# More rows of the gathered table fetched one by one: 36 a group on two issuing engines in place of 8 on one

## The chip, the cores and the metric

The kernel runs on one core of a Trainium2 chip. The metric is the device time of one execution in microseconds (us). Engines: PE = TensorE matmul, PEld = its weight loads, DVE = VectorE, ACT = ScalarE, POOL = GpSimd, SP = SyncE.

## The reference

One layer of graph attention over N = 12500 nodes and 212500 edges (128 features, 8 heads of 16), the edges sorted by their destination:

```python
Q, K, V = x @ WQ, x @ WK, x @ WV                       # N x 128 each, split into 8 heads
Eh = edge_attr @ WE
score = K[src] * Q[dst] / sqrt(16) * Eh                # per edge
score = exp(clip(score.sum(-1), -5, 5))                # one number per edge and head
msg = V[src] * score
h = x + segment_sum(msg, dst) / (segment_sum(score, dst) + 1e-6)
h = batch_norm(h) * gamma + beta
out = layer_norm(x + h)
```

## The kernel before, in words

Edges are cut into 1661 tiles of 128, a row of the chip's 128 partitions for each edge. Eight tiles make a **group** (the last has five); there are 208 groups, each with two windows of up to 64 destination nodes.

**Stage 1** (about the first 80 us) multiplies x with WK and WV and writes the table `kvd` to DRAM: 12500 rows of 1 KB, K and V of a node side by side. Meanwhile POOL gathers rows of x for the first eight groups, which make their K and V themselves.

**Stage 2** is a loop over groups, one iteration per group, software-pipelined by hand: the order of the calls in the loop is the order of the instructions on each engine. For group g the K and V rows of its eight tiles must lie in one of nine buffers (`slot`). They come by indirect DMA issued by POOL (`gather`, L221), one instruction a tile, 128 rows of 1 KB, their numbers taken from `srcs`. A gather for group g + 9 can start when `message(g)` has freed its buffer; in the steady loop gathers are also issued two at a time behind four steps on DVE (`pace`, and `issue`, in the loop).

One iteration on DVE: `products` (L639, K times the query-edge product, two instructions), `scores` (L647), the clip (L657), `both` for the next group (L613), `attn` (L696), `q_rest` (L573), `message` (L663, V times the exponentials), `onehot` (L541 to L544). ACT: `q_hi` (L569, the first part of Q for group g + 3, waits for PE), two exponentials (L658, L659, wait for the clip on DVE), `x_out` (L710), `q_out`, `sums_out`, `eh_out` (L595), `q_window` (L530; every second group a register load of four numbers, L523), `q_mid` (L576). SP loads the edge features of group g + 4 (`ea`, L506, 512 KB, three buffers, so it waits until PE has used group g + 1's), and for every four groups `rbq` (L404).

**Rows one by one.** Of some groups the eighth tile is not gathered by POOL: its 128 rows come by 128 plain DMAs of 1 KB, each with its DRAM address in a register, into a buffer `byrow` of its own (two of them). `row_plan` lists these groups: with n rows fetched an iteration from iteration `FIRST_ROW` on, a tile is complete every 128/n iterations and is used `ROW_LAG` = 2 iterations after its last row was issued. In `fetch_rows` (called once an iteration) SP loads n addresses into registers (L274) and issues n DMAs (L281). They add to one of six semaphores, on which DVE waits in `rows_there` before it uses the tile. Such a group has seven gathers, and its `products`, `scores` and `message` are cut in two, the eighth tile by itself (`parts`).

The loop's start, with the places that the change touches:

```python
    for g in range(NG - 2):
        within(load, g + 4)
        ...
        fetch_rows(g)
        within(q_hi, g + 3)
        within(products, g)
        ...
        within(clip_exp, g)
```

**Stage 3** (about the last 50 us) is the batch norm, the layer norm and the output.

Of the kernel before, what the change touches and what calls it, by code (L numbers as in the profile page):

```python
# [10 lines left out]
U8 = mybir.dt.uint8  # L11
I32 = mybir.dt.int32
# [3 lines left out]
ET = mybir.EngineType  # L16

P = 128
# [4 lines left out]
U = 4  # L23
# [4 lines left out]
EARLY = 3  # L28
RUN = 64
ROWS = P  # L30
FIRST_ROW = 8
LATE = 8
ROW_LAG = 2
SP_ROWS = 8
WORDS = 4
RQ = 4
NSEM = 6
# [40 lines left out]
def gnn_kernel(  # L78
# [31 lines left out]
    consts = ctx.enter_context(tc.tile_pool(name="consts", bufs=1))  # L110
# [129 lines left out]

    by_row, fill = {}, {}
    row_loads = []
    n = SP_ROWS
    row_tiles = row_plan(usizes)
    tot = len(row_tiles) * P
    cols = -(-n // WORDS) * WORDS
    full_rows = tot // n
    blocks = -(-tot // (P * n))
    for q in range(0, full_rows, P):
        row_loads.append((0, q // P * cols, min(P, full_rows - q), n, q * n))  # L250
    if tot % n:
        row_loads.append((full_rows % P, full_rows // P * cols, 1, tot % n, full_rows * n))
    for q in range(-(-tot // n)):
        fill[FIRST_ROW + q] = q
    by_row.update({g: None for g in row_tiles})
    rows_in = [tc.alloc_semaphore(f"rows_in{i}") for i in range(NSEM)]
    row_ids = consts.tile([P, blocks * cols], I32, name="row_ids")
    nc.vector.memset(row_ids, 0)
    kvb = kvd.bitcast(U8).rearrange("n d -> (n d)")

# [1 line left out]
        return [(a, b - 1), (b - 1, b)] if g in by_row and b == G else [(a, b)]  # L262

    def load_row_ids():
        for p, c, m, w, at in row_loads:
            nc.scalar.dma_start(row_ids[p:p + m, c:c + w], bass.AP(
                tensor=rsrc.tensor, offset=rsrc.offset + at, ap=[[n, m], [1, w]]))

    def fetch_rows(g):
        if g not in fill:  # L270
            return
        q = fill[g]
        c = q // P * cols
        _, offs = nc.values_load_multi_w_load_instructions(  # L274
            row_ids[q % P:q % P + 1, c:c + cols], engines=(ET.SP,), min_val=0, max_val=(N - 1) * 8 * P,
            skip_runtime_bounds_check_because="node ids")
        for r, off in zip(range(q * n, min(q * n + n, tot)), offs):
            k = row_tiles[r // P]
            if r % P == 0:
                by_row[k] = rows.tile([P, 1, 2 * P], F32, name="byrow", bufs=2)  # L280
            d = nc.sync.dma_start(by_row[k][r % P:r % P + 1, 0, :].bitcast(U8), kvb[ds(off, 8 * P)].unsqueeze(0))  # L281
# [69 lines left out]
    def within(f, g):  # L351
        return f(g) if 0 <= g < NG else None
# [47 lines left out]
    def load_quad(q):  # L400
        t = late[0].tile([P, RQ, U * P], BF16, name="rbq", bufs=2)
        for h in (0, 1):
            at = ustarts[2 * RQ * q + h] * P
            nc.sync.dma_start(t[h * WN:(h + 1) * WN], bass.AP(  # L404
                tensor=relT.tensor, offset=relT.offset + at, ap=[[0, WN], [G * P, RQ], [1, U * P]]))
        for k in range(RQ):
            RB[RQ * q + k] = t[:, k, :]
# [350 lines left out]
    for q in range(NQ):  # L758
# [13 lines left out]
        k = q - first_step  # L772
# [70 lines left out]
    for g in range(NG - 2):  # L843
        within(load, g + 4)
        within(load_rel, g + 5)
        if (g + 6) % RQ == 0 and (g + 6) // RQ in quads:
            load_quad((g + 6) // RQ)
        fetch_rows(g)
        within(q_hi, g + 3)
        within(products, g)  # L850
        within(q_lo, g + 2)
        within(denom, g - 2)
# [12 lines left out]
        else:  # L865
            left = len(queued)
# [35 lines left out]
        if g == LATE - 2:  # L902
# [3 lines left out]
    g = last - 1  # L906
# [4 lines left out]
                           skip_runtime_bounds_check_because="a count")]  # L911
# [59 lines left out]
    pairs = [[i] for i in range(min(2, NY))] + [list(range(i, min(i + 2, NY))) for i in range(2, NY - 1, 2)]  # L971
# [261 lines left out]
```

## Time and profile before

| what | us |
|---|---|
| median of 3 runs | 2136.09 (2130.42 to 2140.72) |
| the profiled execution: its own time | 2129.71 |
| its span, first to last instruction | 2127.9 |
| busy: PE, DVE, POOL, ACT | 1710.7, 1592.0, 1594.6, 672.2 |
| indirect gathers on POOL | 64 of x, 1585 of `kvd` |
| rows one by one | 1536, that is 12 tiles |

The mean granted TensorE clock of that execution is 0.917. A line of instructions in the profile gives the source line, the engine, the operation, output <- inputs, how many, then busy us, mean ns of one, the idle time just before them, and what ended that idle time. A timeline line gives the start and the duration in us, and in brackets the idle time before it with what ended it ("issue": nothing that the profile shows). "SPq" and "ACTq" are the instructions of the engine's instruction queue: register loads, moves and the issue of DMAs.

### The profile page before, as it was taken

To read this page: it belongs to the slowest core of one execution; us is meant where nothing else is said; L and a number is where in the kernel's file an instruction comes from. 1 tells how busy PE (TensorE), PEld (TensorE's weight loads), DVE (VectorE), ACT (ScalarE), POOL (GpSimd) and SP (SyncE) were. 2 spreads that over 40 slices of the span, in tenths; PEclk is the share of its full clock that TensorE was granted. 3 is DMA by queue.
4 is the path that set the end of the run, shared out by engine and by line. 5 is a ranking of instruction groups with operands and counts; after the bars stand their busy time and mean duration, and the time that the engine had idled before them with its cause. 6 is when DMAs were issued, how large, how long until landed. Compare 5 with 4: busy or idle time off the path is not lost.

```text
span 2127.9 us, 34950 instructions
## 1 busy us (share of the span) xinstructions
PE 1710.7 (80%) x9414; PEld 1105.5 (52%) x9414; DVE 1592.0 (75%) x3593; ACT 672.2 (32%) x2688; POOL 1594.6 (75%) x1685
## 2 busy tenths in 40 slices
PE   8889999777787787787777877787777777777787
PEld 7566566444554454454444554454544444455457
DVE  4559999777777777777777777767777777777687
ACT  3344343322322322322222323223223223223226
POOL 7777777777777777777777777777777777777775
PEclk9999999998998999999898899989898999898889
DMA  9856666565565555565565565565565565565574
GB/s 305 283 183 189 203 198 195 175 175 165 175 176 165 175 177 165 175 178 165 177 174 164 178 175 176 165 175 167 175 178 169 171 177 166 173 180 172 169 237 128
DMA packets 175395, 386.65 MB, mean 182 GB/s; under 512 B 37518, under 2 KB 91831, under 8 KB 175191
## 3 DMA queue, kind: packets, MB, share of 16 engines
q0 software_dynamic: 78128, 212.05, 33.9%
q1 hardware_dynamic: 92900, 169.50, 25.6%
q10 hardware_dynamic: 4163, 2.78, 0.5%
q8 instruction: 78, 1.28, 0.2%
q14 instruction: 126, 1.03, 0.2%
HBM read 364.57 MB, written 19.63 MB: 181 GB/s over the span
## 4 chain that ended last, share of the span: by engine, by line
DVE 32%; DMA 30%; issue 14%; POOL 11%; PE 10%; ACT 1%; DVEq 0%; SPq 0%; POOLq 0%; ACTq 0%
DMA slot<-kvd,srcs 29%; POOL slot L221 11%; DVE s L647 9%; DVE wt L613 6%; DVE slot L639 6%; DVE msg L663 3%; PE ps_a L680 2%; DVE q L579 2%; DVE s L657 1%; PE ps_e L588 1%; PE ps_t L345 1%; DVE rz L692 1%; PE ps_e L725 1%; PE ps_q L725 1%; PE ps_t L621 1%
## 5 line engine op out<-in xcount | busy, mean ns | idle before, releaser
L221 POOL DMA_INDIRECT slot<-kvd,srcs x1585 | 1506.3, 950 | 486.7 <-issue 324.5
L639 DVE TENSOR_TENSOR slot<-slot,ps_t 128x512 f32<-128x512 f32 (+1 forms) x410 | 274.4, 678 | 422.5 <-DMA slot<-kvd,srcs 380.8
L621 PE MATMUL ps_t<-ident,wt 128*128 128x128 f32 x1661 | 282.6, 313 | 365.0 <-DVE wt L613 363.7
L680 PE MATMUL ps_a<-msg,oh 128*128 128x136 f32 (+1 forms) x3322 | 526.5, 298 | 0.5 <-DVE msg L663 0.5
L621 PEld LDWEIGHTS ps_t<-ident,wt 128*128 128x128 f32 x1661 | 212.9, 159 | 538.9 <-issue 472.8
L680 PEld LDWEIGHTS ps_a<-msg,oh 128*128 128x128 f32 (+1 forms) x3322 | 427.6, 171 | 79.5 <-issue 53.4
L658 ACT ACTIVATE ps_m<-s 128x64 f32<-128x64 f32 (+1 forms) x209 | 47.5, 227 | 1095.1 <-DVE s L657 1046.1
L588 PE MATMUL ps_e<-ea,w_e 128*128 128x512 f32 x832 | 390.6, 591 | 0.7 <-ACT wt L595 0.7
L613 DVE TENSOR_TENSOR wt<-wt,ps_q 128x512 f32<-128x512 f32 x416 | 264.6, 676 | 2.6 <-PE ps_q L603 2.6
L663 DVE TENSOR_TENSOR msg<-slot,ps_m 128x1024 f32<-128x1024 f32 (+3 forms) x209 | 246.9, 1183 | 0.4 <-ACT ps_m L658 0.3
L647 DVE TENSOR_REDUCE s<-slot 128x64 f32<-128x1024 f32 (+2 forms) x208 | 246.8, 1187 | 0.1
L595 ACT ACTIVATE wt<-ps_e 128x512 f32<-128x512 f32 x416 | 233.4, 618 | 12.9 <-PE ps_e L588 12.9
L603 PE MATMUL ps_q<-ot,q 64*128 64x512 bf16 x1248 | 210.9, 453 | 0.0
L588 PEld LDWEIGHTS ps_e<-ea,w_e 128*128 128x128 f32 x832 | 142.6, 190 | 100.4 <-issue 98.5
L541 DVE TENSOR_TENSOR oh<-ps_m,rel_i 128x512 f32<-128x512 f32 x208 | 142.0, 683 | 11.2 <-PE ps_a L680 11.2
L569 ACT ACTIVATE q<-qs 128x128 bf16<-128x128 f32 x208 | 64.3, 309 | 216.8 <-PE ps_q L603 183.8
L705 PEld LDWEIGHTS ps_a<-ident,at 128*128 128x128 f32 x408 | 71.3, 218 | 110.8 <-issue 53.5
L705 PE MATMUL ps_a<-ident,at 128*128 128x128 f32 x408 | 114.2, 367 | 2.5 <-DVE relrow L395 2.3
L710 ACT ACTIVATE hx<-ps_a 128x64 f32 x408 | 88.4, 217 | 43.3 <-PE ps_a L680 36.3
L530 ACT ACTIVATE xw<-hx 128x64 f32 x416 | 88.0, 278 | 10.5 <-DMA hx<-xT 10.2
L603 PEld LDWEIGHTS <-q 64*128 64x128 bf16 x1248 | 48.7, 102 | 79.4 <-issue 62.2
L561 PE MATMUL ps_a<-w_q,xw 128*128 128x128 f32 x416 | 88.6, 298 | 0.6 <-ACT qs L565 0.4
(180 smaller groups left out, 1632.6 us busy)
## 6 DMA issues: line engine op xcount, KB each, us to landing
ea<-eaT SPq DMA_DIRECT2D x207, 512.0 KB
slot<-kvd,srcs POOLq DMA_INDIRECT x1585
byrow<-kvd SPq DMA_DIRECT2D x1536, 1.0 KB
rbq<-relT SPq DMA_DIRECT2D x94, 256.0 KB
kvd<-slot SPq DMA_DIRECT2D x12, 512.0 KB
kvd<-t SPq DMA_DIRECT2D x12, 512.0 KB
slot<-xT SPq DMA_DIRECT2D x24, 256.0 KB
out<-o SPq DMA_DIRECT2D x23, 256.0 KB
```

Of the source, the lines that this page charges most:

```text
L221: return nc.gpsimd.indirect_dma_start(out=out, out_offset=None, in_=table, in_offset=bass.IndirectOffsetOnAxis(ap=srcs[:, e:e + 1], axis=0))
L541: nc.vector.tensor_tensor(one, iota_ps[:, None, :].to_broadcast([P, n, P]), r[:, :n, None].to_broadcast([P, n, P]), op=OP.is_equal)
L588: nc.tensor.matmul(eh, w_e, EA[g][:, a:b, :].rearrange("p a b -> p (a b)"), start=True, stop=True)
L595: nc.scalar.activation(t[:, :(b - a) * P], EH[g][h], AF.Copy)
L603: nc.tensor.matmul(QE[g][h], Q3[g][r, k, :], OT[g][r, :(b - a) * P], start=(k == 0), stop=(k == 2))
L613: nc.vector.tensor_tensor(t, t, QE[g][h], op=OP.mult)
L621: nc.tensor.transpose(ps[:, j, :], WT[g][h][:, j * P:(j + 1) * P], ident)
L639: step = nc.vector.tensor_tensor(kv, kv, PW[g][i][:, c - a:d - a, :], op=OP.mult)
L647: step = nc.vector.tensor_reduce(SS[g][:, a:b, :], KV[g](a, b, 0).rearrange("p t (h d) -> p t h d", d=DH), axis=AX.X, op=OP.add)
L663: step = nc.vector.tensor_tensor(MSG[g][:, a:b, :P].rearrange("p t (h d) -> p t h d", d=DH), KV[g](a, b, P).rearrange("p t (h d) -> p t h ...
L680: nc.tensor.matmul(AGG[g][WN if j >= n else 0:], OH[g][j], MSG[g][:, j, :], start=(j == 0), stop=(j == n - 1))
L705: nc.tensor.matmul(ps, AT[g], ident, start=True, stop=False)
```

## The change

36 rows an iteration in place of 8, from iteration 6 in place of 8. SP issues 20 of them where it issued 8; ACT issues the other 16, behind `q_hi` and ahead of the exponentials. `row_plan` then gives 55 tiles in place of 12: groups 11, 15, 18, 22, ... 203 in place of 25, 41, ... 201. POOL gathers 43 tiles fewer. The addresses lie in another order, two fetches to a partition, SP's and ACT's apart.

```diff
-FIRST_ROW = 8
+FIRST_ROW = 6
 LATE = 8
 ROW_LAG = 2
-SP_ROWS = 8
+SP_ROWS = 20
+ACT_ROWS = 16
...
-    full, n = sizes.count(U) // 2, SP_ROWS
+    full, n = sizes.count(U) // 2, SP_ROWS + ACT_ROWS
...
+    def offsets(q, et):
+        c, w, m = (0, sp_step, SP_ROWS) if et == ET.SP else (act_at, act_step, ACT_ROWS)
+        _, offs = nc.values_load_multi_w_load_instructions(
+            row_ids[q // 2:q // 2 + 1, c + q % 2 * w:c + (q % 2 + 1) * w], engines=(et,), min_val=0,
+            max_val=(N - 1) * 8 * P, skip_runtime_bounds_check_because="node ids")
+        return offs[:m]
+
-    def fetch_rows(g):
+    def fetch_rows(g, et, a, b):
         if g not in fill:
             return
-        q = fill[g]
-        c = q // P * cols
-        _, offs = nc.values_load_multi_w_load_instructions(
-            row_ids[q % P:q % P + 1, c:c + cols], engines=(ET.SP,), min_val=0, max_val=(N - 1) * 8 * P,
-            skip_runtime_bounds_check_because="node ids")
-        for r, off in zip(range(q * n, min(q * n + n, tot)), offs):
+        at = fill[g] * n
+        b = min(b, tot - at)
+        if b <= a:
+            return
+        eng = {ET.SP: nc.sync, ET.Activation: nc.scalar}[et]
+        for r, off in zip(range(at + a, at + b), offsets(fill[g], et)):
             k = row_tiles[r // P]
             if r % P == 0:
                 by_row[k] = rows.tile([P, 1, 2 * P], F32, name="byrow", bufs=2)
-            d = nc.sync.dma_start(by_row[k][r % P:r % P + 1, 0, :].bitcast(U8), kvb[ds(off, 8 * P)].unsqueeze(0))
+            d = eng.dma_start(by_row[k][r % P:r % P + 1, 0, :].bitcast(U8), kvb[ds(off, 8 * P)].unsqueeze(0))
...
-        fetch_rows(g)
+        fetch_rows(g, ET.SP, 0, SP_ROWS)
         within(q_hi, g + 3)
+        fetch_rows(g, ET.Activation, SP_ROWS, SP_ROWS + ACT_ROWS)
         within(products, g)
```

What moves, engine by engine. Source lines behind the change stand up to 19 higher than before (L281 is now L299, L569 is L587, L658 is L676).

SP in the middle of the loop, one iteration before the change (`ea` are edge features, `rbq` the loads for four groups, `row_ids` the addresses):

```order
L506 DMA ea<-eaT 128x1024
L404 DMA rbq<-relT 64x4x512 x2
L274 TENSOR_LOAD row_ids
L281 DMA byrow<-kvd 1x1024 x8
L506 DMA ea<-eaT 128x1024
```

and after it:

```order
L524 DMA ea<-eaT 128x1024
L422 DMA rbq<-relT 64x4x512 x2
L282 TENSOR_LOAD row_ids
L299 DMA byrow<-kvd 1x1024 x20
L524 DMA ea<-eaT 128x1024
```

The order is the same; one register load now fills 20 registers, and 20 DMAs stand ahead of the next `ea`.

ACT in the middle of the loop, from `q_mid` to `x_out`, before the change (`q` are the parts of Q, `ps_m<-s` and `msg<-s` the two exponentials):

```order
L576 ACTIVATE q_3251<-qs 128x128
L569 ACTIVATE q_3361<-qs 128x128
L658 ACTIVATE ps_m<-s 128x64
L659 ACTIVATE msg<-s 128x8x8
L710 ISA
L710 ACTIVATE hx<-ps_a 128x64
```

and after it:

```order
L594 ACTIVATE q_4504<-qs 128x128
L587 ACTIVATE q_4711<-qs 128x128
L282 TENSOR_LOAD row_ids
L299 DMA byrow<-kvd 1x1024 x16
L676 ACTIVATE ps_m<-s 128x64
L677 ACTIVATE msg<-s 128x8x8
L728 ISA
L728 ACTIVATE hx<-ps_a 128x64
```

A register load of 16 numbers and 16 DMAs now stand between `q_hi` and the exponentials.

POOL, the gathers of groups 9 to 13, one buffer a row, before the change:

```order
L221 DMA slot_628<-kvd,srcs 128x256 x8
L221 DMA slot_777<-kvd,srcs 128x256 x8
L221 DMA slot_864<-kvd,srcs 128x256 x8
L221 DMA slot_924<-kvd,srcs 128x256 x8
L221 DMA slot_989<-kvd,srcs 128x256 x8
```

and after it:

```order
L222 DMA slot_628<-kvd,srcs 128x256 x8
L222 DMA slot_777<-kvd,srcs 128x256 x8
L222 DMA slot_864<-kvd,srcs 128x256 x7
L222 DMA slot_924<-kvd,srcs 128x256 x8
L222 DMA slot_988<-kvd,srcs 128x256 x8
```

Group 11 has lost a gather; before, group 25 was the first with seven.

More of the change, by code (lines that the diff above doesn't have):

```diff
@@ L242, in gnn_kernel @@
     row_loads = []
-    n = SP_ROWS
+    n = SP_ROWS + ACT_ROWS
     row_tiles = row_plan(usizes)
     tot = len(row_tiles) * P
[L246 to L252, printed above, removed]
+    sp_step = -(-SP_ROWS // WORDS) * WORDS
+    act_at = 2 * sp_step
+    act_step = -(-ACT_ROWS // WORDS) * WORDS
+    pairs = tot // (2 * n)
+    assert pairs < P
+    row_loads.append((0, 0, [[2 * n, pairs], [n, 2], [1, SP_ROWS]], 0, sp_step))
+    row_loads.append((0, act_at, [[2 * n, pairs], [n, 2], [1, ACT_ROWS]], SP_ROWS, act_step))
+    for k in (0, 1):
+        left = tot - 2 * n * pairs - k * n
+        at = (2 * pairs + k) * n
+        for c, a, m in ((k * sp_step, 0, SP_ROWS), (act_at + k * act_step, SP_ROWS, ACT_ROWS)):
+            m = min(m, left - a)
+            if m > 0:
+                row_loads.append((pairs, c, [[1, 1], [1, 1], [1, m]], at + a, m))
     for q in range(-(-tot // n)):
         fill[FIRST_ROW + q] = q
+    cols = act_at + 2 * act_step
     by_row.update({g: None for g in row_tiles})
     rows_in = [tc.alloc_semaphore(f"rows_in{i}") for i in range(NSEM)]
-    row_ids = consts.tile([P, blocks * cols], I32, name="row_ids")
+    row_ids = consts.tile([P, cols], I32, name="row_ids")
     nc.vector.memset(row_ids, 0)
```

8 lines of the change are left out of this document (5 added, 3 removed).

## The prediction

> **What bounds the kernel now.** I read the page first (busy shares, costliest groups), then the waits, then timelines of single engines. On the page these groups matter; the first number behind the bar is busy us, the second the mean ns of one, then the idle time before them.
>
> ```profile
> PE 1710.7 (80%) x9414; PEld 1105.5 (52%) x9414; DVE 1592.0 (75%) x3593; ACT 672.2 (32%) x2688; POOL 1594.6 (75%) x1685
> L221 POOL DMA_INDIRECT slot<-kvd,srcs x1585 | 1506.3, 950 | 486.7 <-issue 324.5
> L639 DVE TENSOR_TENSOR slot<-slot,ps_t 128x512 f32<-128x512 f32 (+1 forms) x410 | 274.4, 678 | 422.5 <-DMA slot<-kvd,srcs 380.8
> L658 ACT ACTIVATE ps_m<-s 128x64 f32<-128x64 f32 (+1 forms) x209 | 47.5, 227 | 1095.1 <-DVE s L657 1046.1
> ```
>
> By share of busy time PE would be the bound. But DVE's one large wait is for gathers (380.8 us), and POOL's idle time, 486.7 us over 1585 gathers, is 0.307 us each, nearly the same ahead of every one. So I looked at POOL in order of time, at three places: early, in the middle, at the end.
>
> ```profile
> 172.20 0.98 POOL L221 DMA_INDIRECT slot<-kvd,srcs  x1 [0.30 <-issue]
> 177.18 0.94 POOL L221 DMA_INDIRECT slot<-kvd,srcs  x1 [4.00 <-DVE msg L663]
> ...
> 1005.27 0.94 POOL L221 DMA_INDIRECT slot<-kvd,srcs  x1 [0.30 <-issue]
> 1006.52 0.96 POOL L221 DMA_INDIRECT slot<-kvd,srcs  x1 [0.30 <-issue]
> ...
> 2074.97 0.95 POOL L221 DMA_INDIRECT slot<-kvd,srcs  x1 [0.30 <-DVE rz L689]
> ```
>
> A gather starts every 1.25 us, waiting for nobody but once: at 177.18 the nine buffers are full and POOL waits 4.0 us for `message` of group 8 to free one. 1585 x 1.25 = 1981 us, and the last gather starts at 2074.97, 53 us before the span ends: **POOL's rate of issuing gathers is the bound**, 10.0 us for eight. How far the other engines are from it is seen where DVE still has gathered groups in store (first row) and in the middle (second row):
>
> ```profile
> 300.00:400.00 100.00, 92.84 (x550) 57.20 (x548) 93.40 (x212) 36.87 (x155) 75.70 (x80) 1.00 0.66 196
> 1000.00:1200.00 200.00, 157.86 (x843) 99.84 (x844) 146.75 (x334) 57.27 (x237) 151.32 (x159) 0.88 0.57 169
> ```
>
> PE and DVE (first and third busy time) are 93% busy in the one and 79% and 73% in the other.
>
> **The gain.** 43 gathers fewer, 43 x 1.25 = 53.8 us. Two of them don't count: those of groups 11 and 15 are issued ahead of the wait at 177.18, which ends when `message(8)` does, so POOL only waits longer. 41 x 1.25 = **51.3 us**. An average iteration then has 8 - 36/128 = 7.72 gathers, 9.65 us. Whether that is had depends on what issues the rows.
>
> **SP.** These are its instructions for a row (min/median/max ns), its register loads of eight numbers and of one, and two stretches of its timeline.
>
> ```profile
> L281 SPq MOVE byrow<-kvd x1536: 29/29/38, 172.4 to 1998.5; - x192
> L281 SPq DMA_DIRECT2D byrow<-kvd x1536: 221/228/310, 172.5 to 1998.5; - x192
> L274 SPq TENSOR_LOAD <-row_ids x192: 698/735/1020, 171.4 to 1995.1; - x192
> L910 SPq TENSOR_LOAD <-bad_i x1: 471/471/471, 2069.4 to 2069.4; - x1
> ...
> 211.01 1.25 SPq L404 DMA_DIRECT2D rbq<-relT  x2
> ...
> 1010.14 0.36 SPq L506 DMA_DIRECT2D ea<-eaT  x1
> 1011.41 2.52 SPq L281 DMA_DIRECT2D byrow<-kvd  x8
> ```
>
> Eight rows take 2.52 us, 0.32 each. From the start of `ea` to the first row is 1.27 us with a load of eight numbers. A load of 20 is not in the trace: from 0.471 (one) and 0.735 (eight) along a line it is 1.19, in proportion to eight 1.84; I take the line, since it has both rows. An iteration of SP is then 1.27 + 0.45 + 20 x 0.32 + 1.25/4 = **8.4 us** (9.1 by the other end), under 9.65. It costs nothing as long as that holds; the next `ea` goes out up to an iteration late, and is used three iterations after its issue. The last rows of a tile are issued two iterations before their use.
>
> **ACT.** It has no such row yet. Its DMAs and register loads (four numbers, one number) are:
>
> ```profile
> L396 ACTq DMA_DIRECT2D relT<-relrow x15: 235/327/586, 32.7 to 1971.5; - x15
> L523 ACTq TENSOR_LOAD <-base_i x104: 304/308/985, 33.8 to 2029.0; - x104
> L910 ACTq TENSOR_LOAD <-bad_i x1: 292/292/292, 2066.9 to 2066.9; - x1
> ```
>
> A row on ACT costs between SP's 0.32 and 0.586 + 0.09 = 0.68 us. ACT's quickest DMA, 0.235 us, is so close to SP's 0.228 that I take 0.32. The load of 16 numbers lies between 0.3 (the line through 0.292 and 0.308 hardly rises) and 16/4 x 0.308 = 1.2; I take 0.45. The block is 16 x 0.32 + 0.45 = **5.6 us**, 11 at the far end. The Trainium skill (DMA: Bandwidth & Descriptors, Latency and other measured facts) gives a `tensor_load` a floor of about 0.6 us; ACT's rows of 0.29 and 0.31 are under it, and by the floor the block would be 5.8.
>
> Behind the block wait both exponentials, and for them `message` on DVE. What covers it is ACT's wait for the clip, from `q_hi` (L569) to the exponential (L658), in iterations 6, 7 and 8, in the stretch bound by DVE, and in the steady one:
>
> ```profile
> 149.81 0.31 ACT L569 ACTIVATE q<-qs 128x128 bf16<-128x128 f32 x1 [0.61 <-PE ps_q L603]
> 151.82 0.23 ACT L658 ACTIVATE ps_m<-s 128x64 f32<-128x64 f32 x1 [1.69 <-DVE rz L692]
> ...
> 164.79 0.31 ACT L569 ACTIVATE q<-qs 128x128 bf16<-128x128 f32 x1 [0.61 <-PE ps_q L603]
> 166.83 0.23 ACT L658 ACTIVATE ps_m<-s 128x64 f32<-128x64 f32 x1 [1.73 <-DVE rz L692]
> ...
> 171.52 0.31 ACT L569 ACTIVATE q<-qs 128x128 bf16<-128x128 f32 x1 [0.61 <-PE ps_q L603]
> 173.83 0.23 ACT L658 ACTIVATE ps_m<-s 128x64 f32<-128x64 f32 x1 [2.00 <-DVE s L657]
> ...
> 213.31 0.31 ACT L569 ACTIVATE q<-qs 128x128 bf16<-128x128 f32 x1 [0.54 <-PE ps_q L603]
> 217.32 0.23 ACT L658 ACTIVATE ps_m<-s 128x64 f32<-128x64 f32 x1 [3.71 <-DVE s L657]
> 220.44 0.31 ACT L569 ACTIVATE q<-qs 128x128 bf16<-128x128 f32 x1 [0.55 <-PE ps_q L603]
> 1003.83 0.31 ACT L569 ACTIVATE q<-qs 128x128 bf16<-128x128 f32 x1 [1.90 <-PE ps_q L603]
> 1009.38 0.23 ACT L658 ACTIVATE ps_m<-s 128x64 f32<-128x64 f32 x1 [5.24 <-DVE s L657]
> ```
>
> ```profile
> 219.19 1.22 DVE L663 TENSOR_TENSOR msg<-slot,ps_m 128x1024 f32<-128x1024 f32 x1
> ```
>
> The windows are 2.0, 2.0, 2.3, 4.0 and 5.5 us. DVE starts `message` 1.6 us after the exponential's end (217.32 to 219.19), busy with other groups' work, so 1.6 us more is covered. From about iteration 15 on, 4.0 + 1.6 = 5.6 covers the block just so; in the steady stretch there is more. If it were not covered, ACT's loop would be 2.6 us (217.32 to 220.44, less the 0.55 wait) plus the block, 8.2 us, still under 9.65. But in **iterations 6 to 8** it sticks out, and `message(8)` frees the buffer for which POOL waits. Iteration 6 loses 5.6 - 2.0 = 3.6 (ACT still makes K and V of group 7 there, so the slack does not help), iteration 7 5.6 - 2.0 - 1.6 = 2.0, iteration 8 5.6 - 2.3 - 1.6 = 1.7: **+7 us** of POOL's wait, once. The bounds are 0 (PE and DVE absorb it) and 11 (a load of 1.2 us: 0.8 to 1.2 more in each).
>
> **DVE.** Each of 43 groups more is cut in two, three times:
>
> ```profile
> L647 DVE TENSOR_REDUCE s<-slot 128x64 f32<-128x1024 f32 x190 | 230.4, 1212 | 0.0
> L647 DVE TENSOR_REDUCE s<-slot 128x56 f32<-128x896 f32 x12 | 12.9, 1077 | 0.0
> L647 DVE TENSOR_REDUCE s<-byrow 128x8 f32<-128x128 f32 x12 | 3.3, 274 | 0.0
> ```
>
> 1.077 + 0.274 - 1.212 = 0.14 us, three times, 0.42 a group, 18 us in all. It lies in DVE's 380.8 us of waiting for gathers and costs nothing; with that cover gone it would cost the 18.
>
> **The sum:** 2129.7 - 51.3 + 7 = 2085.4 on the profiled execution. The median of the runs shown is 6 us higher, within their spread; I predict **2086**, and for this case 2076 (53.8 gained, nothing lost) to 2095.
>
> **Rivals.**
>
> *Two engines issuing at once stretch each row* (slower). No stretch of the trace has SP and ACT issuing single rows together. SP decides first: if it is the bound, the 196 fetches begin near 150 us and the last is used some 80 us before the end (three iterations of 7.1 and the 53 us after the last gather, and a landing), so the time is 230 + 196 S. It passes 2085 at S = 9.46, a row at 0.37 us, and 2130 at S = 9.69, a row at 0.385. At 0.40 S is 10.0 and the time **2190**. On ACT the same happens from 0.41 us a row (block 7.0, loop 9.6). For: SP's margin is only 0.05 us a row, and single issues of 0.31 in place of 0.228 occur. Against: 228 is the median, next to a maximum of 310, while POOL and the `ea` stream run beside it.
>
> *A part of it*: rows at 0.37 to 0.385, or a 1.84 us load besides; the gain is half eaten, 2095 to 2128.
>
> *One DMA engine for all rows* (slower). Each row is one descriptor, and might always go through the same one of the 16 DMA engines. The queues' load:
>
> ```profile
> q0 software_dynamic: 78128, 212.05, 33.9%
> q1 hardware_dynamic: 92900, 169.50, 25.6%
> q10 hardware_dynamic: 4163, 2.78, 0.5%
> ```
>
> 33.9% and 25.6% of 10.0 us are 6.0 us an iteration on each engine. A packet takes 0.5% x 16 x 2128/4163 = 0.041 us (q10, 0.67 KB) to 0.094 (q1, 1.8 KB), and a row of 1 KB lies between: 36 add 1.5 to 3.4 us, 7.5 to 9.4 in all, under 9.65. From 0.10 us a row that engine would set the pace, since every gather ends when its slowest part has landed; at 0.12, 10.3 us, 230 + 196 x 10.3 = 2250. The Trainium skill (DMA: Bandwidth & Descriptors, Why a DMA increments its semaphore by 16 and not by 1) says that a transfer whose outer dimension is 1 uses one engine, on these queues the lowest-numbered. The profile gives only the mean of the 16, so no row here shows it.
>
> *The gathers saved are not on the path*: against it stands POOL's unbroken row of starts; it would give 2130 or, with DVE's 18 us, 2148.
>
> **How the numbers follow.** The forecast has 0.70; part of the gain 0.12; slower by two issuers 0.12, by one DMA engine 0.04; off the path 0.02. The range 2070 to 2125 takes in the first (with the runs' spread of 5 us below) and most of the second. About 0.5%, some 11 us, is what a measurement of this kernel tells from no change: faster by over that 0.78, within it 0.07, slower 0.15.
>
> **What would show it.** Right: 1542 gathers from `kvd`, still 1.25 us apart, the last near 2030; POOL's wait near 177 grown from 4 us to over 10; SP's 20 rows in 6.4 us and ACT's block in 5.6; the exponential's wait shrunk to about 0 to 2 us. Wrong: POOL waiting for `message` all along, SP without idle time, or DVE waiting for rows at L639. What would upset the forecast most is a row that costs 0.06 us more when both queues are in use.

## The result, and the profile after

The changed kernel takes **2136.12 us** (median of 12 runs, 2133.39 to 2141.62) against 2136.47 us for the kernel before (12 runs, 2130.42 to 2140.72): a ratio of 1.0004, 95% interval 0.9993 to 1.0015. No change, where 2086 was predicted. The profiled execution of the changed kernel took 2141.62 us (span 2139.8), 11.9 us more than that of before; these two executions lie at opposite ends of the runs' spread, and a second profile of the changed kernel (2133.67 us) stands beside them below. Some of the runs told below were made under conditions in which the kernel before itself takes 2730 to 2758 us; each ratio is to the kernel before run beside it on the same chip, and those runs stand apart, at the end of the experiments.

On the page of the changed kernel POOL has 43 gathers fewer and still the same end. Its idle time ahead of the gathers has grown from 486.7 to 533.7 us:

```profile
PE 1711.0 (80%) x9414; PEld 1105.5 (52%) x9414; DVE 1598.6 (75%) x3722; ACT 650.0 (30%) x2688; POOL 1559.5 (73%) x1642
L222 POOL DMA_INDIRECT slot<-kvd,srcs x1542 | 1470.7, 954 | 533.7 <-issue 310.7
```

The chain that ended last now runs through the issue of rows on both engines and through the rows' own DMAs, neither of which was among its larger shares before:

```profile
DMA slot<-kvd,srcs 26%; SPq L299 9%; DMA byrow<-kvd 8%; ACTq L299 7%; POOL slot L222 6%; DVE s L665 3%; SPq L282 2%; DVE slot L657 2%; DVE wt L631 2%; PE ps_a L698 2%; PE ps_t L639 2%; DVE msg L681 1%; PE ps_t L363 1%; PE ps_q L621 1%; ACTq L282 1%
```

Where the time went is read best from the count of POOL's instructions in three stretches (200 to 300 us has 80 in both kernels). The count stands behind the fifth busy time, in brackets. First the kernel before, then the changed one:

```profile
100.00:200.00 100.00, 91.94 (x538) 64.53 (x538) 67.45 (x159) 46.15 (x144) 72.85 (x78) 0.97 0.60 184
300.00:1200.00 900.00, 717.82 (x3917) 450.46 (x3916) 686.76 (x1556) 268.19 (x1115) 681.51 (x717) 0.91 0.59 174
1200.00:2000.00 800.00, 624.58 (x3386) 390.96 (x3385) 593.01 (x1330) 233.74 (x972) 605.56 (x639) 0.91 0.58 173
```

```profile
100.00:200.00 100.00, 78.20 (x410) 56.32 (x409) 47.39 (x113) 36.41 (x108) 55.49 (x59) 0.87 0.44 132
300.00:1200.00 900.00, 720.38 (x4010) 455.82 (x4010) 705.81 (x1657) 263.36 (x1141) 657.11 (x690) 0.93 0.64 176
1200.00:2000.00 800.00, 639.06 (x3443) 396.49 (x3441) 604.06 (x1408) 229.35 (x984) 603.35 (x633) 0.92 0.63 176
```

19 gathers fewer fit into the first stretch, 27 into the second and 6 into the third: 52 x 1.25 = 65 us of waiting that were not there before, against 43 x 1.25 = 53.8 us saved. The difference is, within a gather, the 11.9 us by which the last gather starts later (2074.97 before, 2086.9 now).

**The first stretch.** Three waits of POOL make it up; before there was one, of 4.0 us:

```profile
162.66 0.94 POOL L222 DMA_INDIRECT slot<-kvd,srcs  x1 [10.12 <-DVE s L665]
177.74 0.94 POOL L222 DMA_INDIRECT slot<-kvd,srcs  x1 [6.63 <-issue]
198.31 0.94 POOL L222 DMA_INDIRECT slot<-kvd,srcs  x1 [10.77 <-DVE msg L681]
```

Two things stand behind them. The addresses are loaded at 108 us by ACT in five DMAs: two of 97 partitions, which took 1.44 and 3.41 us to issue, and three of one partition, 2.72, 0.24 and 0.26 (before: two, of 128 and 64 partitions, 0.34 and 0.53 us). The Q part and the exponential behind them had to wait. Besides, ACT's block of rows sits between `q_hi` (L587) and the exponential (L676) when nothing covers it:

```profile
108.44 1.44 ACTq L276 DMA_DIRECT2D row_ids<-rsrc  x1
109.93 6.75 ACTq L276 DMA_DIRECT2D row_ids<-rsrc  x4
118.96 0.31 ACT L587 ACTIVATE q<-qs 128x128 bf16<-128x128 f32 x1 [9.68 <-DMA row_ids<-rsrc]
...
161.47 0.31 ACT L587 ACTIVATE q<-qs 128x128 bf16<-128x128 f32 x1 [0.61 <-PE ps_q L621]
162.71 5.32 ACTq L299 DMA_DIRECT2D byrow<-kvd  x16
168.08 0.23 ACT L676 ACTIVATE ps_m<-s 128x64 f32<-128x64 f32 x1 [6.30 <-issue]
```

From 161.47 to 168.08 are 6.6 us; in the same iteration before it was 2.0.

**The second stretch** has no long wait but many short ones. Two rows of POOL's waits in 300 to 1200 us, before and after (in all, times, longest):

```profile
POOL slot L221 <- issue: 139.0, 456, 0.3
POOL slot L221 <- DMA slot<-kvd,srcs: 15.8, 52, 0.3
```

```profile
POOL slot L222 <- issue: 128.5, 407, 2.1
POOL slot L222 <- DMA slot<-kvd,srcs: 37.8, 97, 1.2
```

Before, no wait is over 0.3 us, which is POOL's own pause between gathers. Now it waits up to 1.2 us for *earlier gathers to land*: its gathers take turns on eight semaphores, so each one waits for the gather eight before it, issued 10.0 us earlier. How late they land, the trace's semaphore increments tell. A gather raises its semaphore sixteen times. The trace lacks some increments, so these are medians over the gathers that have at least fourteen of them, in 600 to 900 us, in us after the gather's start:

```
                 last increment but one   last increment
kernel before             2.75                 2.83
changed kernel            3.00                 8.48   (one in ten: 9.9 or more)
```

Fifteen sixteenths come nearly as before and **one comes 5.6 us later**. The same holds for the edge features (`ea`): the last increment but one comes at 4.04 us, the last at 13.23 (before 3.45 and 3.65). One part of sixteen is behind in such transfers. That this is one DMA engine is read from it, and agrees with the rule of the Trainium skill that the prediction named (DMA: Bandwidth & Descriptors, Why a DMA increments its semaphore by 16 and not by 1): it gives a `[1, 1]` transfer to one engine, on these queues the lowest-numbered, and in the trace a row is a `[1, 1]` transfer of 1 KB. No view names the engine.

How much of POOL's loss stands behind a late landing can be counted in the traces. In 300 to 1200 us POOL's starts slip by 36.8 us (counting those over 0.06 us late). Of these, 24.3 us are starts 0.26 or 0.76 us (within 0.02) behind the landing of the gather eight before. Another 8.4 us are seven single starts, each 106 gathers after the one before; five of them stand 3.34 us behind that landing. In the second profile of this kernel, below, it is 18.6 and 8.7 of 32.9 us (at five of the same starts, four of them at 3.34). What is left, 4.1 and 5.6 us, is not much more than all that the kernel before has: 3.9 us, none of it behind a landing. Why every 106th start needs longer, the profile does not say; in the kernel before these starts come 4.1 us or more after the landing, and one of the six there is late, by 0.15 us.

The rows were issued at the pace that was forecast; the loads of their addresses took longer than taken. Minimum, median and maximum in ns:

```profile
L299 SPq DMA_DIRECT2D byrow<-kvd x3920: 217/228/2910, 163.1 to 2048.7; - x196
L299 ACTq DMA_DIRECT2D byrow<-kvd x3120: 226/232/692, 162.7 to 2029.8; - x195
L282 SPq TENSOR_LOAD <-row_ids x196: 1382/1449/1782, 161.4 to 2040.8; - x196
L282 ACTq TENSOR_LOAD <-row_ids x195: 1012/1199/1302, 161.5 to 2023.0; - x195
```

Two things that the prediction had listed as signs of failure are there too: DVE waits for rows, and SP hardly waits for PE any more (1072.1 us before). Beside them DVE waits for ACT's exponentials, 100 times (0.3 us in all before):

```profile
DVE byrow L657 <- DVEq L306: 91.1, 18, 10.4
SPq L524 <- PE ps_e L606: 144.5, 44, 15.3
DVE msg L681 <- ACT ps_m L676: 108.2, 100, 3.4
```

Whether they cost time, these rows do not say; that was the question for the experiments.

### The profile page after: what moved, and what is told of

Same layout as the page of the kernel before. It is cut to its first block, busy times and chain, and to the rows that moved or that the text cites. A ratio compares the mean times of both kernels' runs of the same rounds, so it can differ in the third digit from the quotient of the medians.

```text
span 2139.8 us, 46352 instructions
## 1 busy us (share of the span) xinstructions
PE 1711.0 (80%) x9414; PEld 1105.5 (52%) x9414; DVE 1598.6 (75%) x3722; ACT 650.0 (30%) x2688; POOL 1559.5 (73%) x1642
## 4 chain that ended last, share of the span: by engine, by line
DMA 36%; DVE 13%; SPq 12%; issue 11%; PE 11%; ACTq 8%; POOL 6%; ACT 3%; DVEq 0%; POOLq 0%
DMA slot<-kvd,srcs 26%; SPq L299 9%; DMA byrow<-kvd 8%; ACTq L299 7%; POOL slot L222 6%; DVE s L665 3%; SPq L282 2%; DVE slot L657 2%; DVE wt L631 2%; PE ps_a L698 2%; PE ps_t L639 2%; DVE msg L681 1%; PE ps_t L363 1%; PE ps_q L621 1%; ACTq L282 1%
## 5 line engine op out<-in xcount | busy, mean ns | idle before, releaser
L222 POOL DMA_INDIRECT slot<-kvd,srcs x1542 | 1470.7, 954 | 533.7 <-issue 310.7
L639 PE MATMUL ps_t<-ident,wt 128*128 128x128 f32 x1661 | 261.7, 299 | 258.8 <-DVE wt L631 257.9
L676 ACT ACTIVATE ps_m<-s 128x64 f32<-128x64 f32 (+1 forms) x209 | 47.5, 227 | 1255.1 <-DVE qs L591 374.9
L639 PEld LDWEIGHTS ps_t<-ident,wt 128*128 128x128 f32 x1661 | 204.4, 152 | 416.0 <-issue 341.6
L657 DVE TENSOR_TENSOR slot<-slot,ps_t 128x512 f32<-128x512 f32 (+1 forms) x410 | 261.5, 661 | 203.7 <-DMA slot<-kvd,srcs 155.4
L681 DVE TENSOR_TENSOR msg<-slot,ps_m 128x1024 f32<-128x1024 f32 (+3 forms) x209 | 241.8, 1158 | 105.5 <-ACT ps_m L676 104.8
L665 DVE TENSOR_REDUCE s<-slot 128x64 f32<-128x1024 f32 (+2 forms) x208 | 240.5, 1157 | 0.1
L621 PE MATMUL ps_q<-ot,q 64*128 64x512 bf16 x1248 | 198.8, 430 | 0.0
L579 PE MATMUL ps_a<-w_q,xw 128*128 128x128 f32 x416 | 100.3, 326 | 57.0 <-ACT xw L548 56.1
L579 PEld LDWEIGHTS ps_a<-w_q,xw 128*128 128x128 f32 x416 | 70.6, 212 | 80.5 <-ACT xw L548 78.6
L587 ACT ACTIVATE q<-qs 128x128 bf16<-128x128 f32 x208 | 67.8, 326 | 113.9 <-PE ps_q L621 81.6
L714 DVE SCALAR_TENSOR_TENSOR at<-os,keep,rz 128x128 f32<-128x128 f32 x208 | 71.4, 343 | 33.5 <-PE ps_a L723 32.8
```

What stands on the lines that cost most here:

```text
L222: return nc.gpsimd.indirect_dma_start(out=out, out_offset=None, in_=table, in_offset=bass.IndirectOffsetOnAxis(ap=srcs[:, e:e + 1], axis=0))
L621: nc.tensor.matmul(QE[g][h], Q3[g][r, k, :], OT[g][r, :(b - a) * P], start=(k == 0), stop=(k == 2))
L639: nc.tensor.transpose(ps[:, j, :], WT[g][h][:, j * P:(j + 1) * P], ident)
L657: step = nc.vector.tensor_tensor(kv, kv, PW[g][i][:, c - a:d - a, :], op=OP.mult)
L665: step = nc.vector.tensor_reduce(SS[g][:, a:b, :], KV[g](a, b, 0).rearrange("p t (h d) -> p t h d", d=DH), axis=AX.X, op=OP.add)
L681: step = nc.vector.tensor_tensor(MSG[g][:, a:b, :P].rearrange("p t (h d) -> p t h d", d=DH), KV[g](a, b, P).rearrange("p t (h d) -> p t h ...
```

## The experiments

Theories. **One engine**: all single rows go through one DMA engine, it falls behind, delivers its sixteenth of each gather late, and POOL waits for the gather eight before. **Issuers**: SP (without idle time, 20 rows) and ACT (late with the exponentials, 16 rows) hold the groups back, and the late landing is beside the point. For the first stretch both say the same.

**The changed kernel again.**

> The changed kernel once more, unaltered, in the conditions of the other runs, where the kernel before takes 2734 to 2738 us. One-engine theory and issuer theory alike leave open what it takes there; from the nearest runs (rows from group 10 on: 1.152 to 1.154 of the kernel before) it should take 1.14 to 1.17 of it, if the chip is of that kind, and 0.997 to 1.003 of it, if the kernel before takes 2136 us again.

2135.56 us, ratio 1.0016 (1.0004 to 1.0027): as in the result. Its profile has the same waits: POOL's first stretch, 27.0 us beyond its pace in 100 to 300 us, and 33.3 in 300 to 1200 (27.6 and 38.5 in the first profile).

**Late start, whole rows and half rows.** Both begin the rows at group 10; the row fetches are then 192, two DMAs of 96 partitions load all addresses, and there are 54 tiles.

```diff
-FIRST_ROW = 6
+FIRST_ROW = 10
...
-    row_loads.append((0, 0, [[2 * n, pairs], [n, 2], [1, SP_ROWS]], 0, sp_step))
-    row_loads.append((0, act_at, [[2 * n, pairs], [n, 2], [1, ACT_ROWS]], SP_ROWS, act_step))
+    even = pairs // 16 * 16
+    for p, m in ((0, even), (even, pairs - even)):
+        if m:
+            at = 2 * n * p
+            row_loads.append((p, 0, [[2 * n, m], [n, 2], [1, SP_ROWS]], at, sp_step))
+            row_loads.append((p, act_at, [[2 * n, m], [n, 2], [1, ACT_ROWS]], at + SP_ROWS, act_step))
```

> The change with rows from group 10 on and addresses in pieces of 96 and 1 partitions, whole rows of 1 KB. Where the kernel before takes 2132 to 2137 us: if bytes don't count for the one DMA engine, the same as with half rows, 0.990 of the kernel before (2105 to 2115); if they do, 2116 to 2125. Where it takes 2735 to 2758: 1.15 of it.

With half rows besides:

```diff
-                by_row[k] = rows.tile([P, 1, 2 * P], F32, name="byrow", bufs=2)
-            d = eng.dma_start(by_row[k][r % P:r % P + 1, 0, :].bitcast(U8), kvb[ds(off, 8 * P)].unsqueeze(0))
+                by_row[k] = rows.tile([P, 1, P], F32, name="byrow", bufs=2)
+            d = eng.dma_start(by_row[k][r % P:r % P + 1, 0, :].bitcast(U8), kvb[ds(off, 4 * P)].unsqueeze(0))
...
-                                      by_row[g][:, :, c:c + n])
+                                      by_row[g][:, :, :n])
```

> The change with rows of 512 bytes in place of 1 KB (of a row only the key's half is fetched and stands for the value's half too; the value's half is left out), with rows from group 10 on and with addresses in pieces of 96 and 1 partitions. Both theories: GpSimd's waits of 100 to 200 us fall from 27 us to under 8. One-engine theory: gathers land after 5 to 6 us in place of 8.5 and GpSimd's extra time in 300 to 1200 us falls from 4 to 5 us per 100 us to under 1.5; in all 2136 - 20 - 30 = 2086 (2075 to 2100). Issuer theory: the middle stays as it is: 2115 (2108 to 2125). This holds where the kernel before takes 2132 to 2137 us; where it takes 2735 to 2758, the ratio is 1.15 to 1.17.

Whole rows: 2110.97 us, ratio 0.9893 (0.9869 to 0.9916). Half rows: 2109.91 us, ratio 0.9904 (0.9888 to 0.9921). Whole rows in the three stretches, then half rows in the second:

```profile
100.00:200.00 100.00, 89.40 (x502) 63.23 (x502) 64.00 (x151) 43.23 (x132) 69.80 (x74) 0.94 0.58 170
300.00:1200.00 900.00, 724.35 (x4029) 457.77 (x4028) 712.50 (x1668) 265.93 (x1152) 666.02 (x699) 0.93 0.64 177
1200.00:2000.00 800.00, 635.56 (x3482) 394.25 (x3480) 608.45 (x1416) 230.29 (x992) 602.77 (x635) 0.93 0.63 178
```

```profile
300.00:1200.00 900.00, 729.84 (x4043) 459.67 (x4044) 713.58 (x1674) 266.50 (x1152) 669.00 (x702) 0.94 0.65 176
```

The first stretch has 74 gathers again (59 in the change, 78 before): the early waits were on the path, 15 x 1.25 = 19 us of the 24. Most of the rest of the 25 us by which this kernel is faster than the changed one lies in the second stretch, where it loses 26.3 us against 38.5 and 33.3 in the two profiles of the change. The address loads now take ACT 0.69 and 0.84 us, and POOL's one long wait there is 5.9 us:

```profile
110.96 0.69 ACTq L280 DMA_DIRECT2D row_ids<-rsrc  x1
111.69 0.84 ACTq L280 DMA_DIRECT2D row_ids<-rsrc  x1
```

```profile
180.17 0.94 POOL L222 DMA_INDIRECT slot<-kvd,srcs  x1 [5.94 <-DVE msg L685]
```

How much of the 19 us is the addresses and how much the start was not taken apart. The second stretch stays short of gathers, 699 and 702 against 717: the one-engine forecast for half rows (2086, gathers landing after 5 to 6 us) was missed, and 2109.91 us lies in the range that the issuer theory gave (2108 to 2125). Gathers land after 8.40 us (whole) and 7.93 us (half) in 600 to 900 us, so the bytes of the rows are not what makes their landing late; whole rows came within the range given for that case (2105 to 2115). The waits still stand behind landings: counted as above, 16.0 and 4.8 of 26.0 us with whole rows, 13.3 and 4.0 of 23.3 with half rows.

How late it is, is seen in ACT's rows too, each of which is one packet of 1 KB (or 512 bytes) on ACT's own queue, so that the k-th issue belongs to the k-th packet. A packet of 1 KB takes 46 ns and its semaphore 9. But from issue to the packet's start pass 6.64 us in the changed kernel (median, 600 to 900 us), 6.69 with the late start and 5.35 with half rows. So a row of 55 ns stands in a queue for over 6 us, and halving its bytes shortens that by a fifth. What it stands behind, the gathers' packets of 4 KB with 164 ns each or the other loads, no run shows. By its work that engine is not full: an estimate from these rows is 36 x 0.055 = 2.0 us an iteration beside the 6.0 that the prediction worked out, 8.0 of some 10.

**20 rows by SP alone.** The kernel before with:

```diff
-FIRST_ROW = 8
+FIRST_ROW = 6
...
-SP_ROWS = 8
+SP_ROWS = 20
```

> The kernel before with 20 rows a group by SyncE, none by ScalarE (31 tiles, first rows at group 6). Where the kernel before takes 2132 to 2137 us: if the one DMA engine falls behind only while two engines issue rows together (0.16 us a row, against 0.18 that it can land), one issuer's 0.32 us a row leaves it free: gathers land after 3 to 4 us, GpSimd's extra time in 300 to 1200 us is under 10 us, and 19 gathers x 1.25 = 24 us are saved: 2110 to 2118. If SyncE's 20 rows hold the groups back, the extra time stays near 25 us: 2125 to 2136. Where the kernel before takes 2735 to 2758: 1.11 of it.

2114.09 us, ratio 0.9901 (0.9877 to 0.9924); 31 tiles. Waits and the second stretch:

```profile
SPq L506 <- PE ps_e L588: 150.0, 49, 15.4
```

```profile
DVE byrow L639 <- DVEq L288: 75.4, 12, 12.7
```

```profile
300.00:1200.00 900.00, 733.19 (x4083) 462.86 (x4081) 714.68 (x1648) 286.79 (x1158) 681.75 (x717) 0.92 0.64 180
```

This settles the SP half of the issuer theory, which had forecast 2125 to 2136. SP has as little idle time as in the change (150.0 us of waiting against 144.5), DVE waits for rows nearly as long (75.4 us), and yet POOL issues 717 gathers, as before. Gathers land after 3.23 us, and time and landing are within what the one-engine theory gave. Both signs were harmless by themselves.

**14 rows by SP and 14 by ACT**, with the late start:

```diff
-SP_ROWS = 20
-ACT_ROWS = 16
+SP_ROWS = 14
+ACT_ROWS = 14
```

> 14 rows by SyncE and 14 by ScalarE (some 42 tiles), rows from group 10 on, addresses in pieces of 96 and 1 partitions. Where the kernel before takes 2132 to 2137 us: one-engine theory by two issuers: the bursts overlap for 4.5 us in place of 5.4 to 6.4, gathers land after 5 to 7 us, extra time in the middle 8 to 15 us, 30 gathers x 1.25 = 37.5 saved: 2108 to 2116. SyncE theory: SyncE has 2 us more a group than it needs, extra time under 5 us: 2098 to 2107. Where the kernel before takes 2735 to 2758: 1.02 of it.

**2100.32 us**, ratio 0.9836 (0.9812 to 0.9859): the fastest, 42 tiles. Second stretch, and POOL's waits in it:

```profile
300.00:1200.00 900.00, 735.23 (x4012) 460.55 (x4011) 710.33 (x1646) 267.54 (x1148) 681.79 (x715) 0.92 0.64 179
```

```profile
POOL slot L222 <- issue: 136.1, 446, 0.3
POOL slot L222 <- DMA slot<-kvd,srcs: 25.4, 83, 0.3
```

No wait is over 0.3 us in these rows; 715 gathers. Gathers land after 6.06 us in 300 to 600 us and 3.74 from 600 to 900; an ACT row's packet starts 3.85 and 1.20 us after its issue. So two issuers at once, and a block of 14 rows between `q_hi` and the exponential (DVE waits 43.3 us for exponentials in the whole run), cost POOL hardly anything: 6.9 us in this stretch against 3.7 before. The time is in the range of the SyncE theory (the SP half of the issuer theory: 2098 to 2107) and under that of the one-engine theory (2108 to 2116), which had sized the lateness too large. The SyncE theory itself does not survive the 20 rows by SP.

All kernels in one table: gathers and rows, POOL's time beyond 1.251 us a gather by stretch, and the landing in 600 to 900 us.

| kernel | POOL's gathers of `kvd` | 100 to 300 | 300 to 1200 | 1200 on | last increment |
|---|---|---|---|---|---|
| before | 1585 | 4.6 | 3.7 | 1.7 | 2.83 |
| changed | 1542 | 27.6 | 38.5 | 9.0 | 8.48 |
| late start | 1543 | 9.0 | 26.3 | 7.6 | 8.40 |
| late start, half rows | 1543 | 8.0 | 23.3 | 8.7 | 7.93 |
| 20 by SP | 1566 | 8.1 | 4.6 | 3.4 | 3.23 |
| 14 + 14, late start | 1555 | 8.0 | 6.9 | 5.7 | 3.74 |

By this table the start of the last gather is accounted for: for 14 + 14, 30 x 1.251 = 37.5 saved and 10.6 lost, 26.9; its last gather starts at 2048.1, 26.8 us earlier than before.

**When the wait fades.** DVE has a store of gathered groups at first. In the changed kernel `scores` of a group starts 73 us (median) after the start of the group's last gather in 300 to 400 us, 21 us in 1000 to 1200 and 19 after that; in the kernel before it is 26 us in 300 to 400 and 14 from then on. The slips go with the store: 3 to 6 us per 100 us up to 1000 us in both profiles of the change, at most 2.3 from 1200 on, while the landing falls from 8.5 to some 7 us. With half rows the store is used up by 700 to 800 us, and the slips, up to 7 us per 100 before, are at most 2.6 from there on. With 14 + 14 it is used up by 400 to 500 us.

So the table's last column sets kernels with a store beside kernels without. While it lasts, in 300 to 400 us, gathers land after 7.6 us with 14 + 14 and 8.3 in the change; without it, from 1200 to 1600 us, after 3.7 and 7.1. With 20 rows by SP it is about 3 us all along. The lateness thus grows with the rows with the store and without it, and the wait appears where it nears POOL's 10.0 us.

**Under the other conditions** the kernel before takes 2730 to 2758 us, at a granted clock of about 0.81. What differs is seen with 20 rows by SP, first under those conditions, then under the result's:

```profile
1002.37 10.42 SPq L281 DMA_DIRECT2D byrow<-kvd  x20
1013.50 0.00 SPq L506 DMA_DIRECT2D ea<-eaT  x1
1013.51 1.55 SPq L404 DMA_DIRECT2D rbq<-relT  x2
1016.60 8.96 SPq L281 DMA_DIRECT2D byrow<-kvd  x20
```

```profile
1008.89 6.37 SPq L281 DMA_DIRECT2D byrow<-kvd  x20
1015.36 0.36 SPq L506 DMA_DIRECT2D ea<-eaT  x1
1017.33 6.79 SPq L281 DMA_DIRECT2D byrow<-kvd  x20
```

A row's median issue is 228 ns in both, but here single instructions, register moves too, take 0.7 or 1.4 us now and then (562 of SP's 3970 moves over 0.2 us; in the changed kernel's own trace none of 3922). Twenty rows then take 11.1 us (median, 6.4 under the result's conditions), and SP waits for PE only 35.9 us: there, it seems, every instruction more on an issuing queue is paid. Gathers land after 2.8 to 4.2 us (medians of the few, some 36 to 56 a run, that have fourteen increments in the trace), so the runs say nothing of the theories, and the expectations, where they were written for the result's conditions, fail:

> 20 rows an iteration, all issued by SP from iteration 6, none by ACT: 30 tiles by rows, so 18 gathers fewer than in the kernel before, 22.5 us of POOL's time. Theory ACT (the block of rows on ACT is what ate the gain): ACT is free, so nearly all of it is had, about 2115 us, with gathers still landing late. Theory engine (all rows go through one DMA engine, which is late with its part of every gather): with 20 rows in place of 36 the gathers' last part lands after some 4 to 6 us in place of 8.5, POOL waits for no landing, about 2115 too; the two differ in the landing time. Theory off the path: 2136.

> 36 rows as in the changed kernel, but from iteration 10 on in place of 6 (54 tiles in place of 55), and the addresses come from DRAM by transfers of 96 partitions in place of 97. Theory early (a third of the loss is POOL waiting for buffers before 200 us, since ACT issues address loads for 8 us in iteration 2 and rows while it still makes K and V): POOL's waits before 220 us fall from 26.6 us to under 8, and the time by 15 to 20 us, to about 2118. Theory engine: the early loss goes, but the slow middle stays at some 40 us of POOL waiting, so it stops at 2115 or above. If the middle sets the pace by itself, the time stays near 2136.

> The change with rows of 512 bytes in place of 1 KB: of a row only the key's half is fetched and stands for the value's half too (the value's half is left out). The number of rows, the instructions of SyncE and ScalarE and the work of VectorE stay. One-engine theory: the one DMA engine moves 18 KB a group less, gathers land after 5 to 6 us in place of 8.5, row issues of 0.5 to 2.9 us go away, and most of the 40 us that GpSimd loses between 300 and 1200 us comes back: 2095 to 2112. Issuer theory: SyncE's 20 rows still take 6.4 us and ScalarE's block 6.6: 2130 to 2140.

> The change with rows of 512 bytes in place of 1 KB (of a row only the key's half is fetched and stands for the value's half too; the value's half is left out), with rows from group 10 on and with addresses in pieces of 96 and 1 partitions. The early part and the middle are told apart by the stretches of one trace. Both theories: GpSimd's waits of 100 to 200 us fall from 27 us to under 8. One-engine theory: gathers land after 5 to 6 us in place of 8.5 and GpSimd's extra time in 300 to 1200 us falls from 4 to 5 us per 100 us to under 1.5; in all 2136 - 20 - 30 = 2086 (2075 to 2100). Issuer theory: the middle stays as it is: 2115 (2108 to 2125). This holds on a chip on which the kernel before takes 2132 to 2137 us; on one of the other kind (2735) the ratio is 1.15 to 1.17, as for the change with late rows.

> The change with 14 rows by SyncE and 14 by ScalarE (some 42 tiles), rows from group 10 on and addresses in pieces of 96 and 1 partitions. Both theories relieve the middle: SyncE has 2 us less an iteration, ScalarE 0.6, the one DMA engine eight rows. 30 gathers fewer than before x 1.25 = 37 us, less 5 to 10 us of waits: 2105 to 2112. If a fixed cost comes with ScalarE's issuing at all, 2125 to 2140.

The repeats of the first three had much the same expectations; for 20 rows by SP the issuer theory by then stood at 2120 to 2136.

| kernel | ratio to the kernel before beside it |
|---|---|
| 20 by SP (twice) | 1.1095 (1.1059 to 1.1132), 1.1124 (1.1088 to 1.1160) |
| late start (twice) | 1.1540 (1.1500 to 1.1580), 1.1518 (1.1495 to 1.1542) |
| half rows (three times) | 1.1575 (1.1538 to 1.1613), 1.1613 (1.1587 to 1.1640), 1.1666 (1.1640 to 1.1692) |
| half rows, late start | 1.1629 (1.1590 to 1.1668) |
| 14 + 14, late start | 1.0201 (1.0168 to 1.0235) |

Four kernels ran only there. Rows of four pieces of 256 bytes each, into a buffer with gaps, so that a row would spread over more DMA engines, alone and with the late start:

```diff
-            d = eng.dma_start(by_row[k][r % P:r % P + 1, 0, :].bitcast(U8), kvb[ds(off, 8 * P)].unsqueeze(0))
+            d = eng.dma_start(by_row[k][r % P:r % P + 1, 0, :].rearrange("p (h w) -> p h w", w=72)[:, :, :64].bitcast(U8),
+                              kvb[ds(off, 8 * P)].unsqueeze(0).rearrange("p (h w) -> p h w", h=4))
```

> The changed kernel with each row's 1 KB moved as four pieces of 256 bytes into a destination with gaps, so that one transfer counts four along its outer dimension; DVE reads the eighth tile through the gaps. Theory engine: the pieces go through four DMA engines, each with a fraction of the load; the gathers' last part lands after under 5 us in place of 8.5, POOL's 41 us of waiting between 300 and 1300 us fall under 12, no row's issue takes over 1 us, and the time falls by 25 to 40 us to about 2100. Theory issue (the loss is the time SP and ACT take to issue): the issue of each row gets no cheaper, so the time stays at 2136 or rises to 2150.

> Both: rows in four pieces, from iteration 10, addresses by 96 partitions; 42 gathers fewer than in the kernel before, 52.5 us. Theories engine and early together: the losses go separately, and nearly the whole is had, 2085 to 2095 us. If only one of them is right, the time is that of the better of the two kernels apart, 2100 to 2118. Theory issue: 2130 or more.

Ratios 1.6508 (1.6457 to 1.6559) and 1.6328 (1.6283 to 1.6373). The median issue of a row (the middle one of the three numbers, ns) was 577 on SP and 588 on ACT, against 228 and 232 in one piece:

```profile
L299 SPq DMA_DIRECT2D byrow<-kvd x3920: 3/577/1818, 224.1 to 4429.0; - x196
L299 ACTq DMA_DIRECT2D byrow<-kvd x3120: 2/588/1861, 223.7 to 4378.0; - x195
```

So a row in four pieces costs the issuer 0.35 us more, 7 us in SP's 20. Beside the 8.9 us that SP's iteration takes in the changed kernel that would be well over 9.65, an estimate; under the result's conditions it was not run. The last two edits were to tell ACT's block from the DMA engine, 8 + 16 rows and 18 + 14, both with the late start:

> 8 rows by SyncE and 16 by ScalarE (24 in all, 36 tiles), rows from group 10 on, addresses in pieces of 96 and 1 partitions. ScalarE's block is as long as in the change. Where the kernel before takes 2132 to 2137 us: if ScalarE's block makes the middle's waits, GpSimd's extra time in 300 to 1200 us stays at 25 to 40 us although 12 rows a group are gone: 24 gathers x 1.25 = 30 saved, 2130 to 2145. If the one DMA engine makes them, it has 24 rows, gathers land after 3 to 5 us and the extra time is under 10: 2133 - 30 + 3 = 2106 (2102 to 2114). Where the kernel before takes 2735 to 2758: 1.02 of it or less.

> 18 rows by SyncE and 14 by ScalarE (32 in all, some 48 tiles), rows from group 10 on, addresses in pieces of 96 and 1 partitions. Where the kernel before takes 2132 to 2137 us: one-engine theory: between 28 rows (landing 3.7 to 6 us, no waits) and 36 (8.4 us, waits of 4 us per 100): gathers land after 5 to 7.5 us, extra time 5 to 15 us: 36 gathers x 1.25 = 45 saved, 2095 to 2108. ScalarE theory: its block of 14 cost nothing with 28 rows, so 2133 - 45 + 4 = 2092 (2087 to 2094). Where the kernel before takes 2735 to 2758: 1.05 to 1.12 of it.

Ratios 1.0356 (1.0305 to 1.0408) and 1.0618 (1.0569 to 1.0667): the first missed what was expected there (1.02 or less), the second met it (1.05 to 1.12). Under these conditions the ratio rises with the larger of the two counts of rows, SP's or ACT's: 1.02 with 14, 1.04 with 16, 1.06 with 18, 1.11 and more with 20. What the two kernels take under the result's conditions is not known.

## Why the prediction was wrong, point by point

- **POOL's rate is the bound**: right. 43 gathers fewer at 1.25 us each are 53.8 us, and the account of POOL's starts has them saved. Each of the kernels with 19, 30 and 42 gathers fewer came out faster.
- **SP**: rows at 0.32 us right, 20 in 6.4; the load of 20 numbers took 1.45 us, between the 1.19 taken and the other end, 1.84; the iteration came to 8.9 us (median) and not 8.4. SP without idle time costs nothing, as 20 rows by SP show.
- **ACT's block**: 16 rows at 0.32 right; the load of 16 numbers took 1.20 us where 0.45 was taken, the upper bound that had been worked out in proportion. 6.6 us in place of 5.6. (The 5.8 that stands beside it is 5.7: 16 x 0.32 + 0.6.) Nor did the cover hold it "just so": DVE waited for exponentials 100 times, 1.1 us each. In the middle that cost POOL nothing that can be seen, since what is left of its slips there is not much more than before.
- **The early wait**: mis-sized, 19 gathers or 24 us in place of 7. The block was 1 us longer, and a term was missing altogether: the five address DMAs, 8 us on ACT in place of 0.9. The late start gave 19 us of it back.
- **The failed step** is that the sum has no term for POOL waiting for its own gathers to land. It comes from the rival "One DMA engine for all rows", which got 0.04: the mechanism was named, but weighed as a rate, 7.5 to 9.4 us of work an iteration, under 9.65, so no harm. The price was looked for in the engine's share and not in its delay. The last part of each gather lands 5.6 us later, and POOL has only 10.0 us from a gather to the one that reuses its semaphore, of which landing used 2.8 before. At 8.5 us (9.9 for one in ten) it waits again and again. Where 51.3 - 7 = 44 us of gain were forecast, the table's rows give 23 us lost before 300 us (27.6 against 4.6), 35 from 300 to 1200 (38.5 against 3.7) and 7 after (9.0 against 1.7): 65 us against 53.8 saved.
- **Two engines issuing stretch each row**: did not come. The median row stayed at 228 and 232 ns; a few SP rows took up to 2.9 us.
- **The gathers saved are not on the path**: this rival named about the time that came (2130), but not for its reason. With 19 gathers fewer (20 by SP) the kernel is 19 us faster, with 30 (14 + 14) 33 us.
- **DVE's 18 us more**: hidden, as forecast; its busy time grew by 6.6 us, and it still waits 155.4 us for gathers.
- The other signs: the last gather was to start near 2030 and starts at 2086.9. DVE's waiting for rows was listed as a sign of failure; with 20 rows by SP it is there, 75.4 us, and costs nothing.

**What stays open**: what a row queues behind, and why the lateness shrinks when DVE's store is used up. What DVE's waits for rows and exponentials would cost if the gathers landed early is open too: from 300 to 1200 us of the changed kernel DVE waits 80.7 us for rows, 67.9 for exponentials and only 19.5 for gathers, since it lives on its store. No run under the result's conditions has ACT's block of 16 rows with fewer rows in all. That it is not what holds POOL up in the middle rests on the place of the slips in the traces alone.

## What to carry to other kernels

Price a shared queue by its delay as well as by its load: ask which wait sits at the end of the transfer and how much time it has left (here 10.0 us from a gather to the next use of its semaphore). Here single-row DMAs made one of the sixteen parts of every wide transfer late, and a wide transfer ends with its last part; halving their bytes hardly helped. And a change of this kind is best swept: 28 rows a group beat 8 by 1.6%, and 36 with the same late start by 0.5% (2100.32 against 2110.97 us, run side by side).

## What the runs showed of the hardware

- One of a gather's sixteen increments came 5.5 us behind the last but one (8.48 against 3.00 us) with a mean DMA share of only 0.64 in that stretch.
- Halving a row's bytes (1 KB to 512) changed the kernel's time by 1 us, the landing of gathers by 0.5 us (600 to 900 us) and a row's stay in ACT's queue from 6.69 to 5.35 us.
- Two address loads of 97 partitions cost ACT 1.44 and 3.41 us to issue, and one of a single partition behind them 2.72; two of 96 partitions cost 0.69 and 0.84.
- A register load takes 0.31 us for four numbers and 1.20 for 16 on ACT; 0.74 for 8 and 1.45 for 20 on SP.
- A row's DMA in four pieces takes SP 0.577 us to issue, in one piece 0.228.
- Under some conditions the same program takes 28% longer, with single instructions of 0.7 to 1.4 us on SP's and ACT's queues; there 8 rows a group were the best of those tried. What brings these conditions about was not found.
